# Score rows stored as single words, reciprocals on GpSimd, and 23 more products in three passes, in a four-layer graph network under a planned order

## The chip, the cores and the metric

The kernel runs on one core of one Trainium2 chip. Its time is the device time of one launch in microseconds. Before the change the median of three runs is 1486.99 us (1486.86 to 1487.59).

## What is computed

The input x has 32 graphs of 512 nodes with 128 features; one weighted adjacency matrix of 512 x 512 serves all graphs. Four layers follow each other, each of the form x = x + layer(relu(layernorm(x))). All of it is in fp32.

```python
# layer 0: graph convolution
A_norm = d[:, None] * (adj + I) * d[None, :];  out = (A_norm @ h) @ W.T + b
# layer 1: gated graph network, 5 steps; both of its matrices are adj
m_in = adj @ h;  av = concat([m_in, m_in]);  u3 = h @ u3_w.T + u3_b
z = sigmoid(av @ w3_w.T + w3_b + u3)
r = sigmoid(av @ w4_w.T + w4_b + u3)
hv = tanh(av @ w5_w.T + w5_b + (r * h) @ u5_w.T + u5_b)
h = (1 - z) * h + z * hv
# layers 2 and 3: graph attention
h = x @ W;  e = leaky_relu((h @ a_src)[:, None] + (h @ a_dst)[None, :])
alpha = softmax(where(adj > 0, e, -inf));  out = alpha @ h      # layer 2: elu(out)
```

## The kernel before

One graph's 512 x 128 tile is the unit: 128 partitions by four chunks of 128, 512 words in a partition, which is also one of the eight PSUM banks. Products come in two forms. A plain fp32 product (`weigh`, L829) is one call that the trace shows as two MATMUL records. A split product cuts both operands into an `upper` and a `lower` part and a scaled combination `across` of the two, held in the type float32r, and runs three single passes in place of one plain product (`one_pass`, L832; `in_three`, L713). The function `operands` (L683 to L692) makes the three parts of a tile: one ACT instruction for `upper` (L686), one DVE instruction for `lower` (L687) and one for `across` (L689). The parts have 5, 5 and 6 buffers. Between the first two passes and the third the partial sum in the bank is rescaled once by ACT (`rescale`, L695).

A step of layer 1 (`step`) starts a bank named `gate` with the state's product with the u3 weights and adds the message's product with the w4 weights. For the pairs (graph, step) that are in `STATE_GATES` (L31) the state's product too is run in three passes, with parts from `operands(hT, ...)`; for others it is one `weigh` from `hT`, issued with the third pass of the message. Steps 2 and 3 of the graphs 2 to 31 are in the set, and step 1 for graphs with b % 4 == 1: 67 products. The message's parts are made in every split step, so the rescaling of the bank is there in either case.

An attention layer of one graph (`gat`) normalises x, turns it through DRAM (`shuttle`), multiplies it by the weights with three score columns appended (L962), and takes the exponentials of the scores of two chunks at a time into the last three columns of `h_gat` (L978); ACT then scales the features by the first of them (L982). The column D + 2 of all 512 nodes is needed as a row in each partition. For graphs 0 to 27 DVE transposes the last 32 columns in 32 x 32 blocks into `four` (L998), one DMA issued by SP writes every 32nd partition of it to the DRAM tile `line` (L1000), and a second one reads `line` into all partitions of `row` (L1002). DVE multiplies and masks to the weights `e` (L1005, four instructions), and PE mixes the features with them (L1031), with the sum of the weights in the last column of each of two banks. DVE takes the reciprocals of two chunks' sums out of the bank (L1034) and ACT scales the bank by them into `v` (L1038); with that the bank is free. The last four graphs ("near") have their rows turned on PE and finish on DVE. A layer's result is added to x by an accumulating DMA that GpSimd issues (L658).

No loop sets the order. Every operation is first entered with `op(engine, cost, due, emit, r=, w=)`: an estimated cost, a due time, and what it reads and writes. `Plan.run` then simulates the engines as queues with these costs: a ready operation with the smallest due time starts when its engine is free and its buffers are there, and a buffer comes free with its last use. Ten rounds are made for each pair in the `ends` of the plan (L373), the best is kept, and `nudge` then moves due times by amounts that follow from the list `NUDGES`. The order in which operations started is the order in which each engine's instructions are emitted; on the chip each engine takes its instructions strictly in that order and waits by semaphores. SP (which issues nearly all DMAs) and GpSimd (POOL) are such queues too. So a changed cost, operation, end or nudge gives another order of the whole program.

Of the kernel before, what the change touches and what calls it, by code (L numbers as in the profile page):

```python
# [14 lines left out]
ALU = mybir.AluOpType  # L15

P = 128
# [3 lines left out]
W = 32  # L21
Q = P // W
# [5 lines left out]
RUN_UP = 8  # L28
LANES = 6
WHOLE_GATES = {(0, 0), (1, 0)}  # L30
STATE_GATES = {(b, s) for b in range(2, 32) for s in (1, 2, 3) if s > 1 or b % 4 == 1}  # L31

NUDGES = (
    53937, 420269, 836905, 654738, 2556, 688223, 875681, 275050, 155096, 344911, 330173, 435081, 694231, 213763,
    619624, 447574, 890946, 78316, 123147, 852796, 311235, 532539, 705019, 644762, 122001, 254734, 428857,
    882175, 724559, 991387, 688947, 809908, 194618, 494830, 529850, 799901, 343325, 398127, 50886, 241542,
    734658, 18633, 943566, 750849, 361157, 207391, 729651, 26139, 37696, 408480, 215591, 995383, 816582, 584268,
    494753, 34361, 342059, 302953, 168035, 239750, 279141, 68953, 280704, 389122, 194085, 766091, 380916,
    187191, 889942, 112078, 155070, 333073, 736484, 517839, 70535, 334845, 651590, 758394, 921455, 429200,
    648202, 752373, 775521, 430492, 606178, 231202, 882688, 679159, 354420, 928437, 520287, 661997, 81128,  # L40
    762603, 72380, 63081, 983120, 327354, 210125, 648122, 266391, 656086, 635831, 781379, 551997, 170768,
    229958, 7605, 122665, 19790, 73379, 142730, 998949, 708013, 923384, 153267, 690409, 481837, 535551, 726547,
    6387, 549650, 56134, 483951, 926497, 198992, 426418, 278155, 699450, 83978, 319322, 141756, 196198, 650583,
    862777, 201601, 166009, 204473, 988478, 570561, 164420, 526913, 618467, 275849, 776494, 261229, 110220,
    498182, 380461, 378001, 220860, 670765, 118796, 827070, 785629, 894747, 990151, 807156, 873672, 718913,
    239396, 50887, 63051, 862147, 532718, 800211, 505997, 9798, 801159, 13694, 618014, 193111, 44188, 893667,
    599496, 714567, 888600, 835938, 364887, 158288, 309678, 793120, 699620, 516755, 592013, 992036, 487540,
    190584, 971338, 58993, 486501, 268529, 250721, 557238, 569064, 166944, 933806, 390862, 463360, 136662,
    215430, 595978, 384591, 96926, 326923, 708222, 859934, 514585, 669817, 296375, 269747, 738262, 834297,
    459159, 608570, 133902, 490320, 941827, 144497, 573319, 819458, 309171, 845111, 880350, 927808, 432234,  # L50
    556385, 655493, 972795, 866892, 892882, 338341, 731096, 806800, 593721, 754374, 280850, 287395, 593450,
    812363, 340434, 322205, 340551, 845735, 66582, 645768, 736844, 878238, 109388, 497625, 999333, 437014,
    859840, 92294, 458622, 403652, 881921, 496809, 361450, 302403, 643048, 262383, 321316, 875159, 728173,
    763887, 249514, 200508, 52886, 149934, 537415, 299931, 655951, 358934, 513673, 678761, 726703, 828099,
    359414, 939210, 916234, 209320, 71814, 960653, 167324, 81204, 557783, 235008, 861486, 815903, 314980,
    593693, 811661, 356673, 912853, 833145, 889341, 728473, 302959, 14483, 119625, 907405, 192404, 98679, 42557,
    675297, 874633, 738462, 562610, 653446, 648327, 99334, 956314, 305909, 318958,
)


# [261 lines left out]
def gnn_stack(ctx: ExitStack, tc: tile.TileContext, a: dict, out: bass.AP):  # L322
    nc = tc.nc
    x, adj = a["x"], a["adj"]
    B, N, D = x.shape
    C = N // P
# [6 lines left out]
    def tiles(n, shape, name, pool=sb, dtype=F32):  # L333
        return [pool.tile(shape, dtype, name=f"{name}_{next(serial)}") for _ in range(n)]

    def flat(t):
# [19 lines left out]
        "hv": tiles(0, TOKENS, "hv"),  # L356
        "gT": tiles(0, [P, Q, W * C], "gT"),
        "h_gat": tiles(3, [P, C, D + 3], "h_gat"),
        "four": tiles(2, [P, Q, W], "four"),
        "row": tiles(2, [P, N], "row"),  # L360
        "line": tiles(4, [C, Q, W], "line", dram),
        "e": tiles(2, [P, C, N], "e"),
# [7 lines left out]
        "rstd": tiles(8, SMALL, "rstd"),  # L370
        "off": tiles(6, SMALL, "off"),
        "rden": tiles(3, SMALL, "rden"),
    }, [(167, 0.1), (181, 0.05)], 12,  # L373
        IDLE_FROM, lambda v: nc.tensor.transpose(v.t[:, 0, :], ident.t, ident.t))
    op = plan.op
    MM, MM1, TURN, MR = 0.858, 0.224, 0.111, 0.2325
# [44 lines left out]
    for c in range(C):  # L421
        e, q = (("ACT", nc.scalar), ("SP", nc.sync))[c % 2]
# [26 lines left out]
    for c in range(C):  # L449
        p = Val("bank")  # L450
# [90 lines left out]
    for i, l in enumerate((2, 3)):  # L541
        p = Val("bank")
# [398 lines left out]
    def gat(b, l, due):  # L941
# [45 lines left out]
        if near:  # L987
            pr = Val("bank")

            def spread():  # L990
                for k in range(Q):
                    nc.tensor.transpose(pr.t[:, k, :], h.t[:, k, D + 2:D + 3].to_broadcast([P, P]), ident.t)  # L992
            op("PE", C * TURN, due + 2, spread, r=[*exps, ident], w=[pr, e])
            row = pr
        else:

            four, line = Val("four"), Val("line")
            op("DVE", 0.2, due + 1.5, lambda: nc.vector.transpose(  # L998
                four.t, h.t[:, :, D + 3 - W:]), r=[h], w=[four])
            op("SP", 0.4, due + 1.5, lambda: nc.sync.dma_start(  # L1000
                line.t, four.t[W - 1::W]), r=[four], w=[line], delay=2.5)
            op("SP", 0.4, due + 1.5, lambda: nc.sync.dma_start(  # L1002
                row.t, line.t.rearrange("c q i -> (c q i)").unsqueeze(0).to_broadcast([P, N])), r=[line], w=[row, e], delay=7)
        for j in range(C):
# [4 lines left out]
        apart = near and l == 3 and b == B - 1  # L1009
        per = 1 if apart else 2  # L1010
        ps, rden, v, n = [Val("bank") for _ in range(C // per)], Val("rden", C), Val("y", 2), Val("r", 2)
        if near:

            def mix_from(js, cs):
                for j in js:
                    for c in cs:
                        nc.tensor.matmul(flat(ps[c // per].t).rearrange("p (c k) -> p c k", c=2)[:, c % per, :D + 1],  # L1017
                                         e.t[:, j, c * P:(c + 1) * P], h.t[:, j, :D + 1], start=j == 0 and c % per == 0,
                                         stop=j == C - 1, skip_group_check=True)
            for js, cs in [([j], range(C)) for j in range(2 if apart else C)] + [((2, 3), [c]) for c in range(C if apart else 0)]:  # L1020
                op("PE", len(js) * len(cs) * MM1, due + 4, lambda js=js, cs=cs: mix_from(js, cs),
                   r=[part for j in js for part in (e[j], h[j // 2], h[2 + j // 2])], w=[*ps] if len(js) == 1 else [ps[cs[0]]])
        for a, p in enumerate(ps):
            pt = lambda p=p: flat(p.t).rearrange("p (c k) -> p c k", c=2)
            chunks = range(per * a, per * a + per)
            some = slice(chunks[0], chunks[-1] + 1)
            for c in range(2 if not near else 0):
                def mix(a=a, c=c, pt=pt):
                    i = 2 * a + c
                    for j in range(C):  # L1030
                        nc.tensor.matmul(pt()[:, c, :D + 1], e.t[:, j, i * P:(i + 1) * P], h.t[:, j, :D + 1],  # L1031
                                         start=(j == 0), stop=(j == C - 1))
                op("PE", C * MM1, due + 4, mix, r=[e, h], w=[*ps] if a == c == 0 else [p])
            op("DVE", 0.08, due + 4, lambda some=some, pt=pt: nc.vector.reciprocal(rden.t[:, some], pt()[:, :per, D]), r=[p], w=[rden[c] for c in chunks])  # L1034
            if not near:
                def divide(chunks=chunks, pt=pt):
                    for c, i in enumerate(chunks):
                        nc.scalar.activation(v.t[:, i, :], pt()[:, c, :D], AF.Identity, bias=3.0 - l, scale=rden.t[:, i:i + 1])  # L1038
                op("ACT", 0.52, due + 4, divide, r=[p, *(rden[c] for c in chunks)], w=[v[a]])
            elif l == 2:  # L1040
                op("DVE", 0.335, due + 4, lambda some=some, pt=pt: nc.vector.tensor_mul(
                    v.t[:, some], pt()[:, :, :D], rden.t[:, some, None].to_broadcast([P, 2, D])), r=[p, rden[2 * a], rden[2 * a + 1]], w=[v[a]])
            else:
                def finish(chunks=chunks, pt=pt):
                    for c, i in enumerate(chunks):
                        nc.vector.scalar_tensor_tensor(xb.t[:, i, :], pt()[:, c, :D], rden.t[:, i:i + 1], xb.t[:, i, :],
                                                       op0=ALU.mult, op1=ALU.add)
                op("DVE", per * 0.26, due + 4, finish, r=[p, *(rden[c] for c in chunks)], w=[xb[c] for c in chunks])
# [77 lines left out]
```

## Time and profile before

| | |
|---|---|
| median of three runs | 1486.99 us |
| the profiled execution | 1487.39 us |
| its span, first to last instruction | 1485.6 us |
| granted TensorE clock | 1.000 |
| DMA packets on the hardware queue q1 | 276160, 41.6% of the 16 DMA engines' span |
| DMA packets on the software queue q0 | 30912, 16.3% |
| DMAs issued for `line`, each 2.0 KB | 56 |
| DMAs issued for `row`, each 256.0 KB | 56 |
| reciprocals out of two-chunk and one-chunk banks (L1034) | 130, 112 of them for graphs 0 to 27 |

The 1.8 us between the span and the time of the profiled execution lie outside the instructions. PE, DVE, ACT and POOL are the four computing engines; PEld is PE's weight load, which runs beside its matmuls. A MATMUL's duration in the records is not its cost, because matmuls are pipelined; the distance from one start to the next is.

### The profile page before, as it was taken

How to read it: one execution, taken by the hardware profiler on the slowest of the kernel's cores; microseconds unless marked ns; L12 is line 12 of the kernel's file. 1: busy time of each engine (PE TensorE's matmuls, PEld its weight loads, DVE VectorE, ACT ScalarE, POOL GpSimd, SP SyncE). 2: the span in 40 equal slices, each digit the busy share in tenths (PEclk: the TensorE clock that was granted, in tenths of full speed). 3: DMA queues.
4: the chain of work that ended last, by engine and by line, in shares of the span. 5: the costliest groups of instructions: out<-in, count | busy, mean ns of one | idle time of the engine just before them, and what ended most of it. 6: DMA issues, size and time to landing. Idle time of an engine off the chain costs nothing.

```text
span 1485.6 us, 25858 instructions
## 1 busy us (share of the span) xinstructions
PE 1478.1 (99%) x7481; PEld 1171.1 (79%) x7481; DVE 1406.2 (95%) x2951; ACT 1271.5 (86%) x2858; POOL 662.5 (45%) x1270
## 2 busy tenths in 40 slices
PE   9999999999999999999999999999999999999999
PEld 7777777787777788778778787877777877778888
DVE  8989999999998999899999999999999999999998
ACT  6978998888988888988889989799888889988874
POOL 5613641333755363655455553366536632414221
PEclk9999999999999999999999999999999999999999
DMA  3445555666766666666766557676576665553233
GB/s 107 65 104 144 108 127 117 139 142 159 154 136 134 156 156 138 139 142 138 178 138 145 134 128 153 143 173 139 127 162 154 148 158 122 136 135 74 70 79 79
DMA packets 307502, 196.12 MB, mean 132 GB/s; under 512 B 87872, under 2 KB 259232, under 8 KB 307360
## 3 DMA queue, kind: packets, MB, share of 16 engines
q1 hardware_dynamic: 276160, 157.24, 41.6%
q0 software_dynamic: 30912, 36.71, 16.3%
q8 instruction: 59, 0.97, 0.3%
q14 instruction: 83, 0.68, 0.2%
q10 hardware_dynamic: 288, 0.52, 0.1%
HBM read 87.30 MB, written 70.37 MB: 106 GB/s over the span
## 4 chain that ended last, share of the span: by engine, by line
PE 97%; DVE 1%; ACT 0%; DMA 0%; issue 0%; ACTq 0%; DVEq 0%
PE bank L713 35%; PE bank L832 26%; PE bank L829 15%; PE bank L1031 13%; PE bank L962 4%; PE bank L791 2%; PE bank L1017 2%; PE bank L736 1%; PE bank L653 0%; DVE e L1005 0%; DMA e<-in_adj_dram 0%; PE bank L507 0%; PE bank L992 0%; DVE st L630 0%; PE bank L455 0%
## 5 line engine op out<-in xcount | busy, mean ns | idle before, releaser
L695 ACT ACTIVATE bank<-bank 128x512 f32<-128x512 f32 x662 | 381.1, 598 | 92.4 <-PE bank L713 56.8
L689 DVE SCALAR_TENSOR_TENSOR across<-lower,upper 128x512 fp32r<-128x512 f32 x413 | 276.5, 678 | 2.2
L832 PE MATMUL bank<-upper,gates 128*128 128x512 f32 x541 | 257.2, 475 | 0.0
L1031 PEld LDWEIGHTS bank<-h_gat,e 128*128 128x128 f32 x1792 | 218.3, 191 | 17.6 <-issue 9.8
L1031 PE MATMUL bank<-h_gat,e 128*128 128x129 f32 x1792 | 220.5, 275 | 0.0
L832 PE MATMUL bank<-across,gates 128*128 128x512 f32 x541 | 218.3, 445 | 0.1
L832 PE MATMUL bank<-lower,gates 128*128 128x512 f32 x541 | 214.1, 396 | 0.0
L658 POOL DMA_DIRECT2D x<-y x80 | 72.1, 905 | 311.4 <-DVE y L1061 88.1
L713 PE MATMUL bank<-adj,upper 128*128 128x512 f32 x640 | 185.8, 412 | 0.0
L713 PE MATMUL bank<-adj,across 128*128 128x512 f32 x640 | 183.8, 411 | 0.0
L713 PE MATMUL bank<-adj,lower 128*128 128x512 f32 x640 | 172.7, 391 | 0.0
L829 PE MATMUL bank<-r,wT 128*128 128x512 f32 x320 | 163.3, 592 | 0.0
L1005 DVE SCALAR_TENSOR_TENSOR e<-row,h_gat,maskT 128x512 f32<-128x512 f32 x224 | 156.9, 741 | 0.0
L568 POOL TENSOR_TENSOR apart<-st 128x4 f32<-128x4 f32 x104 | 53.7, 517 | 218.1 <-DVE st L580 216.1
L713 PEld LDWEIGHTS bank<-adj,across 128*128 128x128 f32 x640 | 117.1, 188 | 36.6 <-issue 8.1
L713 PEld LDWEIGHTS bank<-adj,upper 128*128 128x128 f32 x640 | 117.8, 188 | 34.7 <-issue 10.3
L713 PEld LDWEIGHTS bank<-adj,lower 128*128 128x128 f32 x640 | 120.2, 188 | 26.6
L832 PEld LDWEIGHTS bank<-upper,gates 128*128 128x128 f32 x541 | 102.0, 188 | 42.5 <-issue 14.6
L832 PEld LDWEIGHTS bank<-across,gates 128*128 128x128 f32 x541 | 100.3, 188 | 41.1 <-issue 10.1
L874 ACT ACTIVATE r<-bank,gate_bw 128x512 f32<-128x512 f32 x160 | 111.4, 699 | 24.1 <-PE bank L829 21.4
L832 PEld LDWEIGHTS bank<-lower,gates 128*128 128x128 f32 x541 | 102.1, 189 | 37.8 <-issue 19.1
L568 POOL TENSOR_TENSOR rstd<-rstd,mhalf 128x4 f32<-128x4 f32 x104 | 128.1, 1232 | 5.1
(168 smaller groups left out, 3317.1 us busy)
## 6 DMA issues: line engine op xcount, KB each, us to landing
far<-sq SPq DMA_DIRECT2D x936, 64.0 KB
h<-far SPq DMA_DIRECT2D x148, 256.0 KB
x<-y POOLq DMA_DIRECT2D x80, 256.0 KB, 4.2
sq<-far SPq DMA_DIRECT2D x56, 256.0 KB
row<-line SPq DMA_DIRECT2D x56, 256.0 KB
adjT<-y POOLq DMA_DIRECT2D x32, 256.0 KB, 4.3
hT<-far SPq DMA_DIRECT2D x120, 64.0 KB
x<-in_x_dram SPq DMA_DIRECT2D x24, 256.0 KB
```

The source lines that it names most:

```text
L568: op("POOL", cost, due, lambda: nc.gpsimd.tensor_tensor(to(), one(), other(), how), r=r, w=w)
L658: op("POOL", 1.0, due, lambda: nc.gpsimd.dma_start(x.t, what(), accum_op=ALU.add), r=reads, w=[x], delay=7)
L689: op("DVE", V, due - 5, lambda: nc.vector.scalar_tensor_tensor(flat(across.t), flat(lower.t).bitcast(F32), -SPLIT, flat(upper.t).bitcast(F ...
L695: op("ACT", COPY, due, lambda: nc.scalar.mul(flat(p.t), flat(p.t), by), w=[p])
L713: nc.tensor.matmul(flat(p.t), left.t[:, c, :], right.t[:, c, :], start=first and c == 0, stop=c == C - 1, skip_group_check=True)
L791: nc.tensor.matmul(p.t[:, c, :], m.t[:, c, :], w0T.t[:, 0, :], start=True, stop=True)
L829: nc.tensor.matmul(flat(p.t), (of or gates).t[:, i, :], flat(moving.t), start=start, stop=True, skip_group_check=True)
L832: nc.tensor.matmul(flat(p.t), of.t[:, i, :], flat(moving.t), start=start, stop=True, skip_group_check=True)
L874: op("ACT", A, due - 5, lambda: nc.scalar.activation(flat(r.t), flat(gate.t), AF.Tanh, bias=gate_b["w4"].t, scale=0.5), r=[gate, gate_b["w ...
L962: nc.tensor.matmul(qt()[:, c, :D + 3], gT.t[:, 2 * a + c, :], w_aug[l].t, start=True, stop=True)
L1005: op("DVE", 0.661, due + 3, lambda j=j: nc.vector.scalar_tensor_tensor(e.t[:, j, :], matrix(row), h.t[:, j, D + 1:D + 2], mask.t[:, j, :], ...
L1031: nc.tensor.matmul(pt()[:, c, :D + 1], e.t[:, j, i * P:(i + 1) * P], h.t[:, j, :D + 1], start=(j == 0), stop=(j == C - 1))
```

## The change

Three things change, and the plan's ends and nudges with them.

1. `STATE_GATES` takes in step 1 for all graphs from 2 to 31: 90 products in place of 67. Each of the 23 new ones goes through `operands(hT, ...)` and three passes in place of one `weigh`.
2. The block transpose and `four` are gone. Four DMAs, one for each group of 32 partitions, take column D + 2 straight from `h_gat`, a word at a time (32 partitions by 4 words), into the four parts of `line`. They wait for the exponentials (`exps`) alone and not for the scaled features.
3. For graphs 0 to 27 ACT copies the two sums of a bank to an SBUF tile `den` (of the kind `ve`), GpSimd raises them to the power -1 into `rden`, and ACT's scaling waits for that. For the near graphs the DVE reciprocal stays.

```diff
-STATE_GATES = {(b, s) for b in range(2, 32) for s in (1, 2, 3) if s > 1 or b % 4 == 1}
+STATE_GATES = {(b, s) for b in range(2, 32) for s in (1, 2, 3)}
 NUDGES = (
-    53937, 420269, 836905, 654738, 2556, 688223, 875681, 275050, 155096, 344911, 330173, 435081, 694231, 213763,
...
+    527448, 875016, 948027, 354677, 457100, 447574, 546624, 346310, 530559, 796649, 845369, 700889, 705707,
...
-        "four": tiles(2, [P, Q, W], "four"),
...
-    }, [(167, 0.1), (181, 0.05)], 12,
+    }, [(156.9, 0.133)], 12,
...
-            four, line = Val("four"), Val("line")
-            op("DVE", 0.2, due + 1.5, lambda: nc.vector.transpose(
-                four.t, h.t[:, :, D + 3 - W:]), r=[h], w=[four])
-            op("SP", 0.4, due + 1.5, lambda: nc.sync.dma_start(
-                line.t, four.t[W - 1::W]), r=[four], w=[line], delay=2.5)
+            line = Val("line", C)
+            for c in range(C):
+                op("SP", 0.44, due + 1.5, lambda c=c: nc.sync.dma_start(
+                    line.t[c].rearrange("q i -> i q"), h.t[c * W:(c + 1) * W, :, D + 2]), r=exps, w=[line[c]], delay=3)
...
+        if not near:
+            den = Val("ve", 2)
...
-            op("DVE", 0.08, due + 4, lambda some=some, pt=pt: nc.vector.reciprocal(rden.t[:, some], pt()[:, :per, D]), r=[p], w=[rden[c] for c in chunks])
+            if not near:
+                op("ACT", 0.1, due + 4, lambda some=some, pt=pt: nc.scalar.copy(den.t[:, some], pt()[:, :per, D]), r=[p], w=[den[a]])
+                op("POOL", 1.15, due + 4, lambda some=some: nc.gpsimd.tensor_tensor(
+                    rden.t[:, some], den.t[:, some], minus1.t[:, some], ALU.pow), r=[den[a], minus1], w=[rden[c] for c in chunks], delay=1)
+            else:
+                op("DVE", 0.08, due + 4, lambda some=some, pt=pt: nc.vector.reciprocal(rden.t[:, some], pt()[:, :per, D]), r=[p], w=[rden[c] for c in chunks])
```

`NUDGES` is replaced as a whole by another list (315 numbers before, 186 after).

## The prediction

> **What bounds the kernel now.** I read the page's shares first, then the waits of PE, then the chain of waits, then the groups by shape, then the timeline where a duration was not a cost.
>
> ```profile
> PE 1478.1 (99%) x7481; PEld 1171.1 (79%) x7481; DVE 1406.2 (95%) x2951; ACT 1271.5 (86%) x2858; POOL 662.5 (45%) x1270
> PE 97%; DVE 1%; ACT 0%; DMA 0%; issue 0%; ACTq 0%; DVEq 0%
> ```
>
> PE is busy for all but 7.5 us and makes 97% of the chain that ended last; DVE is close behind with 95%. The waits of PE by itself begin like this, and its six rows sum to 4.0 us, most of it at the start:
>
> ```profile
> PE bank L411 <- DVE r L404: 1.1, 1, 1.1
> PE bank L1017 <- DVE e L1005: 0.9, 2, 0.6
> ```
>
> So the end moves with the sum of PE's passes and with nothing else, as long as PE stays fed. At most about 4 us can be won by a better order alone, and all of 4.0 plus any new wait can be lost. The chain of waits in a stretch of the middle gives the cost of each product:
>
> ```profile
> 603.66 0.86 PE bank L829 x2
> 604.52 0.48 PE bank L832 x2
> 605.86 1.86 PE bank L832 x8
> 608.66 1.87 PE bank L832 x8
> ```
>
> A plain product (two records) takes 0.86 us, a single pass 0.233. The groups by shape give the pieces that the change touches:
>
> ```profile
> L1034 DVE RECIPROCAL rden<-bank 128x2 f32<-128x2 f32 x126 | 18.0, 156 | 1.0 <-PE bank L1031 0.8
> L998 DVE STREAM_TRANSPOSE four<-h_gat 128x128 f32<-128x128 f32 x56 | 16.7, 298 | 2.9 <-ACT h_gat L982 2.9
> L978 ACT ACTIVATE h_gat<-bank 128x6 f32<-128x6 f32 x112 | 19.6, 190 | 4.9 <-PE bank L962 4.7
> L611 POOL TENSOR_TENSOR rstd<-rstd,mhalf 128x3 f32<-128x3 f32 x1 | 0.9, 866 | 5.8 <-DVE rstd L609 5.8
> L611 POOL TENSOR_TENSOR rstd<-rstd,mhalf 128x1 f32<-128x1 f32 x1 | 0.7, 682 | 0.0
> ```
>
> These means overlap from one instruction to the next. What an engine really gives to each is the distance of starts in the timeline of DVE:
>
> ```profile
> 310.16 0.30 DVE L998 STREAM_TRANSPOSE four<-h_gat 128x128 f32<-128x128 f32 x1
> 310.39 0.65 DVE L890 SCALAR_TENSOR_TENSOR hT<-r,r 128x512 f32<-128x512 f32 x1
> ...
> 312.75 0.68 DVE L687 TENSOR_TENSOR lower<-hT,upper 128x512 fp32r<-128x512 f32 x1
> 313.35 0.68 DVE L687 TENSOR_TENSOR lower<-h,upper 128x512 fp32r<-128x512 f32 x1
> 313.95 0.68 DVE L890 SCALAR_TENSOR_TENSOR hT<-r,r 128x512 f32<-128x512 f32 x1
> ```
>
> A block transpose costs 0.23 us, a 512-wide instruction 0.60. A reciprocal at 1468.95 is followed by the next start at 1469.03: 0.08. DVE's margin by stage:
>
> ```profile
> 600.00:800.00 200.00, 200.00 (x986) 157.57 (x986) 190.50 (x375) 178.18 (x399) 104.69 (x197) 1.00 0.65 146
> 1200.00:1400.00 200.00, 200.00 (x978) 156.40 (x977) 193.02 (x372) 175.11 (x388) 59.70 (x116) 1.00 0.49 119
> ```
>
> The fourth figure is DVE: 7 to 10 us free in 200, ACT (the fifth) 22 to 25, POOL about half.
>
> **What the Trainium skill says.** "FP8 and Floating Point Precision", TensorE Precision Notes, has a true fp32 product as four passes; the trace agrees (0.86 is 3.7 passes of 0.233). "PSUM — Partial Sum Buffer", The four PSUM rules, says that GpSimd cannot touch PSUM; so the sums must first be copied by ACT, and no row of this trace has a POOL instruction on a bank. "DMA: Bandwidth & Descriptors", Rules for kernel authors, says that a strided last dimension becomes one descriptor per element; the word columns will then be 512 packets for a row, which no run here shows yet. "Perfetto Trace Analysis", GPSIMD Engine Instruction, calls POOL's spans unreliable and the spacing of starts better; the trace agrees (spans on POOL overlap at 608.15 to 610.82).
>
> **Part 1, 23 products in three passes.** On PE each removes 0.86 and adds 3 x 0.233 = 0.70: 0.16 saved, 3.7 us in all. Taken over the whole span, L832 has 26% of 1485.6 us for 3 x 541 passes, 0.238 each, which includes small gaps: 0.146 saved, 3.4 us. I take 0.152: **3.5 us off PE's sum**, and since PE is the chain, off the end. The price is 23 more instructions on ACT (0.51 each by starts at 619.84 and 620.35: 11.7 us) and 46 on DVE (0.60 each: 27.6 us). The rescaling of the bank is there already. The parts need one more set of upper, lower and across buffers per product: 436 sets in place of 413 (DVE's L689 has x413), 6% more turnover.
>
> **Part 2, words in place of the transpose.** DVE loses 56 x 0.23 = 12.9 us. SP has 224 issues where it had 56, 168 more at 0.43 (128 words a piece at 8.5 to 14 us) to 0.50 (L1000): 72 to 84 us. It issues some 1,440 DMAs now, at about 0.46 some 660 us, so it goes from 45 to 50% of the span. Behind the four issues on SP stand the writes and reads of the shuttles, each 1.5 us later than it could be at most, 56 times. The wait moves from DVE's transpose (SP stands 81.3 us for it in 22 waits) to the exponentials, which ACT ends a scaling earlier, so SP is held less. The packets are 56 x 512 = 28,672 more. The queue's mean packet costs 41.6% x 16 x 1485.6 / 276160 = 0.036 us of one DMA engine; at that price they add 64 us to the 16 engines' mean, 4% of the span; at the least almost nothing. I take 2%. The row arrives within about a microsecond of when it did: three more issues (1.4 us) against the transpose, its wait and the scaling saved. DVE never stood idle ahead of L1005, so I cost the row at nothing; the six interleaved graphs of work hide it. If that cover were gone, 56 x 1 us would be the scale.
>
> **Part 3, reciprocals by GpSimd.** DVE loses 112 x 0.08 = 9.0 us. DVE in sum: 27.6 - 12.9 - 9.0 = +5.7 us of 79 free: it gets no closer to being the bound (95.0%). ACT gets 112 copies of 128 x 2 out of a bank, like L978: between 0.05 (starts 620.35, 620.40) and 0.19 each, 6 to 21 us; with part 1 it goes from 1271 to about 1296, 87%. POOL gets 112 powers of two columns; L611 with one and three columns brackets them at 0.68 and 0.87, I take 0.78: 87 us, 45 to 51%. The bank waits for copy, power and scaling in place of reciprocal and scaling: at least 1 us longer. At 621.66 the reciprocal is done and the scaling starts at 623.39, since ACT has other work queued, so 1 us fits into waits that are there now. New waits: POOL's power stands for ACT's copy, and behind it norms and accumulating DMAs; ACT's scaling stands for POOL, and behind it ACT's rescalings (L695), for which PE waits.
>
> **The new order.** Other ends and nudges reshuffle everything. Below: it could win up to 3 us of the 4.0 that PE waits, not the start. Above: no reason excludes a loss. I take nothing, because the plan's costs matched the chip well enough in the kernel before to leave PE hardly a wait between 50 and 1400 us, and the same costs stand in the new plan.
>
> **The sum.** 1487.39 (profiled) - 3.5 = 1483.9; the profiled execution lies 0.4 above the median, so the forecast for the median is **1483.5**, 0.24% less. About 0.2%, 3.0 us, is what a measurement of this kernel tells from no change; the line is at 1484.0, close to my forecast.
>
> **Rivals.**
> 1. PE loses part of the gain to small waits. For: DVE and ACT both get fuller, with 23 more sets of parts in unchanged buffers. Against: there is no such wait now. With 0.5 to 6.5 us of waits, 1484.0 to 1490.0; at 2.5, 1486.0.
> 2. ACT is held at its scaling by GpSimd. POOL's norm runs as a string of ten instructions, from 624.65 to 631.45 in the timeline, and POOL stands up to 34 us for the data of an accumulating DMA (L658). A power queued behind either comes late, ACT stands, the rescalings behind it come late, and PE stands for the third pass. For: ACT already waits 14.2 us for the reciprocals of DVE. Against: POOL is half idle and the order is made with its queue in it. If one scaling in ten (11 of 112) costs PE 1 us, 1483.5 + 11 = 1494.5. It decides for slower from 6.5 us of PE waits on, 58 ns for each reciprocal.
> 3. The order gets tighter as well: 3.5 + 2.5 less, 1481.0. For: DVE is rid of 168 instructions that broke its rows. Against: PE has no wait left to give in the middle.
> 4. The change doesn't do what it says because plain products stay in the trace: then 1487.0. The diff leaves no room for it.
>
> **How the numbers follow.** The forecast with PE as full as now 0.46, rival 1 0.28, rival 2 0.22, rival 3 0.04, rival 4 nothing. Faster is forecast and rival 3, 0.50; within 0.2% is rival 1, 0.28; slower is rival 2, 0.22. The forecast's own range is 1482.5 to 1484.0 (the bounds of 0.146 and 0.16 per product and a spread of 0.5). The range to hold 8 in 10 goes from 1480.5, below rival 3, over all of rival 1 to 1491.5, into the mild third of rival 2; some 0.15 is left out above.
>
> **What would show it.** L829 from hT falls from x186 by 46 records to x140, and L832 rises from x541 to x564 for each part. PE's busy time falls by 3 to 4 us and its share stays at 99%. DVE stays at 95%; POOL goes to about 51%. ACT's waits for `rden` on POOL stay below some 30 us in all; if they are above 60 us and PE's waits grow, rival 2 is right. Waits of PE on parts (L686 to L689) or on `e` speak for rival 1. Packets of 4 bytes on q1 rise by 28,672 with less than 5% more share. I am wrong if PE's waits exceed 8 us, or if its passes take another time than 0.86 and 0.233.

## The result, and the profile after

The changed kernel takes 1627.8 us, median of four runs (1621.63 to 1633.24), beside 1487.2 us (1486.86 to 1487.59) for the kernel before: a ratio of 1.0945, 95% interval 1.0918 to 1.0971. It is 140.6 us slower, where 3.5 us less had been forecast. The profiled execution has 1626.86 us and a span of 1625.0. Line numbers in the changed code are about ten less than before (the third pass L832 is now L822, the plain product L829 is L819, the DMA that reads the row L1002 is L991).

These are the shares, the main DMA queue and the chain's shares, from the page of the changed kernel:

```profile
PE 1523.2 (94%) x7502; PEld 1197.1 (74%) x7502; DVE 1416.1 (87%) x2829; ACT 1293.4 (80%) x2993; POOL 751.9 (46%) x1382
...
q1 hardware_dynamic: 307968, 157.25, 41.5%
...
PE 19%; DMA 17%; ACT 7%; DVE 7%; SPq 5%; issue 2%; DVEq 0%; ACTq 0%
```

PE made 97% of the chain. Now the chain can be followed back only to 697.85 us, so its shares sum to 57% of the span; PE makes 19 of these and DMA 17. No engine has become the bound: all four have a smaller share than PE had, DVE and ACT smaller ones than their own before. The share that might have warned, that of the DMA engines, is where it was (41.6%). But it is a share of a longer span: as busy time, 41.6% of 1485.6 us are 618 us and 41.5% of 1625.0 are 674. PE's busy time grew by 45 us, although the new products should have made it 3.5 us less. The clock, which was granted at 0.98 over the span and at 1.000 before, may have a part in that: two per cent of 1625 us, 32 us, is an upper estimate.

In the two stretches by stage that the prediction used (us, then PE, PEld, DVE, ACT, POOL, the clock, the DMA share, GB/s) PE, DVE and ACT are emptier, POOL is fuller, in one stretch the clock falls to 0.95, and less is moved in a microsecond than before (129 and 117 GB/s for 146 and 119):

```profile
600.00:800.00 200.00, 188.10 (x915) 147.03 (x914) 175.17 (x328) 164.34 (x380) 116.23 (x196) 0.98 0.65 129
1200.00:1400.00 200.00, 177.87 (x807) 136.52 (x806) 165.94 (x307) 149.82 (x338) 80.16 (x166) 0.95 0.54 117
```

The waits of PE (us in total, times, longest) were six rows with 4.0 us in all. Now 22 rows make about 98 us, and they begin like this:

```profile
PE bank L952 <- DMA sq<-far: 19.4, 10, 5.3
PE bank L819 <- DMA hT<-far: 14.7, 3, 7.0
PE bank L822 <- ACT bank L685: 13.5, 8, 4.1
```

PE waits for data from the shuttles through DRAM, which the change did not touch, and for ACT, which waits for such data in its turn. So look at the queue that issues all these transfers. The waits of SP in the changed kernel:

```profile
SPq L991 <- DMA line<-h_gat: 169.3, 63, 6.7
...
SPq L989 <- ACT h_gat L968: 55.7, 21, 11.3
```

SP stands 169.3 us ahead of the row's DMA (L991) until the words have landed in `line`. In the kernel before the same wait, for a block in place of words, was 22.4 us in 18 waits:

```profile
SPq L1002 <- DMA line<-four: 22.4, 18, 2.6
```

The timeline of SP in the changed kernel shows one such row:

```profile
452.49 1.64 SPq L989 DMA_DIRECT2D line<-h_gat  x3
454.18 0.43 SPq L657 DMA_DIRECT2D far<-sq  x1
454.66 0.85 SPq L989 DMA_DIRECT2D line<-h_gat  x1
455.55 0.47 SPq L408 DMA_DIRECT2D x<-in_x_dram  x1
462.85 0.34 SPq L991 DMA_DIRECT2D row<-line  x1
```

The last of the four word DMAs is issued by 455.51, and the read of the row only at 462.85. In between SP issues nothing for 6.8 us. In the kernel before, the read of a row came 2.80 us after the block's DMA, with four other issues between:

```profile
216.00 0.62 SPq L1000 DMA_DIRECT2D line<-four  x1
...
218.80 0.40 SPq L1002 DMA_DIRECT2D row<-line  x1
```

But SP's standing is not all. The chain that ended last (start, us, what) holds transfers of other tiles as long as that:

```profile
768.91 7.67 DMA h<-far
...
798.21 7.20 DMA line<-h_gat
826.71 7.34 DMA line<-h_gat
...
871.21 7.44 DMA hT<-far
```

`h<-far` and `hT<-far` are plain shuttle reads. Either the words slow down whatever is under way with them, or these reads were merely issued into a crowd. That became the question for the experiments, beside the two others that the prediction left: GpSimd's reciprocals and the order.

### The profile page after: what moved, and what is told of

Same layout as the page of the kernel before. It is cut to its first block, busy times and chain, and to the rows that moved or that the text cites. A ratio compares the mean times of both kernels' runs of the same rounds, so it can differ in the third digit from the quotient of the medians.

```text
span 1625.0 us, 26265 instructions
## 1 busy us (share of the span) xinstructions
PE 1523.2 (94%) x7502; PEld 1197.1 (74%) x7502; DVE 1416.1 (87%) x2829; ACT 1293.4 (80%) x2993; POOL 751.9 (46%) x1382
## 3 DMA queue, kind: packets, MB, share of 16 engines
q1 hardware_dynamic: 307968, 157.25, 41.5%
## 4 chain that ended last, share of the span: by engine, by line
PE 19%; DMA 17%; ACT 7%; DVE 7%; SPq 5%; issue 2%; DVEq 0%; ACTq 0%
DMA line<-h_gat 7%; PE bank L703 5%; PE bank L822 5%; PE bank L1022 3%; DMA h<-far 3%; PE bank L819 3%; DMA far<-sq 2%; PE bank L1008 2%; ACT bank L685 2%; DMA hT<-far 1%; SPq L657 1%; DMA row<-line 1%; DVE lower L677 1%; SPq L989 1%; PE bank L952 1%
## 5 line engine op out<-in xcount | busy, mean ns | idle before, releaser
L679 DVE SCALAR_TENSOR_TENSOR across<-lower,upper 128x512 fp32r<-128x512 f32 x436 | 290.7, 678 | 4.0 <-PE bank L822 1.4
L822 PE MATMUL bank<-upper,gates 128*128 128x512 f32 x564 | 264.9, 470 | 6.6 <-ACT bank L685 2.8
L822 PE MATMUL bank<-across,gates 128*128 128x512 f32 x564 | 225.2, 446 | 19.4 <-ACT bank L685 10.7
L1022 PEld LDWEIGHTS bank<-h_gat,e 128*128 128x128 f32 x1792 | 226.6, 195 | 19.3 <-issue 5.5
L822 PE MATMUL bank<-lower,gates 128*128 128x512 f32 x564 | 227.1, 403 | 9.6 <-DVE lower L677 9.6
L1022 PE MATMUL bank<-h_gat,e 128*128 128x129 f32 x1792 | 230.6, 279 | 1.9 <-DVE e L994 1.9
L703 PE MATMUL bank<-adj,across 128*128 128x512 f32 x640 | 191.5, 425 | 10.8 <-ACT bank L685 10.5
L1027 POOL TENSOR_TENSOR rden<-ve,minus 128x2 f32<-128x2 f32 x112 | 106.2, 977 | 179.4 <-ACT ve L1026 176.2
L819 PE MATMUL bank<-r,wT 128*128 128x512 f32 x320 | 164.2, 595 | 2.4 <-DVE r L866 2.4
L676 ACT ACTIVATE upper<-h 128x512 fp32r<-128x512 f32 x158 | 100.6, 638 | 69.0 <-DMA h<-far 63.2
L558 POOL TENSOR_TENSOR apart<-st 128x4 f32<-128x4 f32 x104 | 70.3, 677 | 179.8 <-DVE st L570 179.1
L822 PEld LDWEIGHTS bank<-across,gates 128*128 128x128 f32 x564 | 105.1, 192 | 60.2 <-ACT bank L685 20.0
L677 DVE TENSOR_TENSOR lower<-h,upper 128x512 fp32r<-128x512 f32 x158 | 107.2, 680 | 45.7 <-ACT upper L676 43.4
L822 PEld LDWEIGHTS bank<-upper,gates 128*128 128x128 f32 x564 | 108.2, 192 | 52.3 <-ACT bank L685 14.6
L822 PEld LDWEIGHTS bank<-lower,gates 128*128 128x128 f32 x564 | 108.3, 192 | 50.1 <-issue 16.5
```

Of the source, the lines that this page charges most:

```text
L558: op("POOL", cost, due, lambda: nc.gpsimd.tensor_tensor(to(), one(), other(), how), r=r, w=w)
L676: op("ACT", COPY, due - 5, lambda: nc.scalar.mul(made(upper.t), given(src.t), BELOW), r=[src], w=[upper])
L677: op("DVE", V, due - 5, lambda: nc.vector.tensor_sub(made(lower.t), given(src.t), made(upper.t).bitcast(F32)), r=[src, upper], w=[lower])
L679: op("DVE", V, due - 5, lambda: nc.vector.scalar_tensor_tensor(flat(across.t), flat(lower.t).bitcast(F32), -SPLIT, flat(upper.t).bitcast(F ...
L703: nc.tensor.matmul(flat(p.t), left.t[:, c, :], right.t[:, c, :], start=first and c == 0, stop=c == C - 1, skip_group_check=True)
L819: nc.tensor.matmul(flat(p.t), (of or gates).t[:, i, :], flat(moving.t), start=start, stop=True, skip_group_check=True)
```

## The experiments

**Theories.** A: a DMA of single words takes long to land, and that alone (times 56, through SP and through what waits) makes the loss. B: GpSimd holds ACT at its scaling (the prediction's second rival). C: the planned order no longer fits, since it was made with a landing of 3 us for the words. Within A: is it the number of words, of DMAs, or the place they are written to; and is it SP's wait or the transfers themselves?

**Landing alone.** A kernel of its own that computes no layer; it stores a row in several ways on SP's queue and reads it back with a DMA that must wait for the store, once with idle DMA engines and once behind eight 64 KB stores of ACT's queue. A DMA has landed when its semaphore says that all of it has arrived; SP issues the read only then, so the time from issue to issue measures the landing.

```python
sync.dma_start(line["block"], four[W - 1::W])                                       # L55, 4 runs of 512 B
sync.dma_start(line["one"][0].rearrange("q i -> i q"), S[:W, :, D + 2])              # L60, 128 words
sync.dma_start(line["few"][0, :, :4].rearrange("q i -> i q"), S[:4, :, D + 2])       # L76, 16 words
```

> No layer is computed; the output is the input. The kernel only stores scores to DRAM in several forms, each followed by a read of what was stored, which SP can issue only when the store has landed; eight times each, first with nothing else under way, then behind eight 64 KB DMAs of another queue. Words theory: the block form (4 runs of 512 B) lands in about 2 us as before, one DMA of 128 single words in clearly more, four of them in 6 to 7 us or more, and 16 words are as fast as the block; then the number of single words is the cost. Rival, the number of DMAs: one DMA of 128 words lands like the block, and four only 1.5 us later (three more issues). Rival, GpSimd: all forms land in about 2 us and the 6 us seen in the changed kernel come from queueing behind other DMAs, so they show only in the loaded half.

The timeline of SP in this kernel, each store with the read after it:

```profile
31.06 0.50 SPq L55 DMA_DIRECT2D lineblock<-four  x1
32.64 0.32 SPq L56 DMA_DIRECT2D R<-lineblock  x1
...
57.71 0.32 SPq L60 DMA_DIRECT2D lineone<-S  x1
64.79 0.32 SPq L61 DMA_DIRECT2D R<-lineone  x1
```

From issue to issue the block takes 1.66 us (median), one DMA of 128 words 6.4 (5.5 to 8.0), the four of a row 7.9 from the first and 6.6 from the last, 16 words 1.2, and 32 runs of 16 bytes 1.66. The eight big stores beside them change no median by more than 0.53 us. So the landing of words takes 4.7 us longer than a block's by itself, without contention (4.2 beside the stores), and it doesn't add up over four DMAs: they land together.

**The changed kernel with fewer words.** Its order, queues and number of DMAs are kept; each word DMA moves 16 words in place of 128, and the rest of the row holds leftovers (GpSimd writes them once at the start, here and in the later runs with leftovers).

```diff
-  line.t[c].rearrange("q i -> i q"), h.t[c * W:(c + 1) * W, :, D + 2])
+  line.t[c][:, :4].rearrange("q i -> i q"), h.t[c * W:c * W + 4, :, D + 2])
```

> The changed kernel with its order kept to the instruction, and each of the four score DMAs moving 16 words in place of 128; the other words of the row are leftovers, so the weights are computed from other numbers. SP's queue, its waits on the exponentials and the number of DMAs stay. Words theory: SP stands some 10 us for line in place of 169 us, and the time falls to 1484 to 1500 us. Rival, the four DMAs themselves and the ring of DMA semaphores: 1580 to 1630 us. Rival, GpSimd's reciprocals hold ACT: 1600 to 1630 us with ACT's and POOL's waits as they are.

It takes 1488.76 us in one run, with 1487.78 for the kernel before beside it. Its page, and SP's wait ahead of the row:

```profile
PE 1476.7 (99%) x7502; PEld 1176.0 (79%) x7502; DVE 1410.0 (95%) x2829; ACT 1290.5 (87%) x2993; POOL 777.0 (52%) x1386
...
SPq L992 <- DMA line<-h_gat: 11.0, 22, 1.4
```

With the same 224 DMAs, the same GpSimd reciprocals, the same 90 products and the same nudged order, the whole loss but about a microsecond is gone. That leaves little to B, and to C only what the order can't stand once words land late.

**Each part alone, both in an order without nudges.** The kernel before with `NUDGES = ()` is their base; one adds the words, the other the reciprocals by copy and GpSimd, and both keep the 67 products.

> The kernel before with an empty list of nudges: what an order costs that has not been nudged, as the base for the parts that are run alone without nudges. All theories: 1495 to 1515 us.

> The kernel before, without nudges, with the score row as single words alone (reciprocals on DVE, 67 products in three passes). Words theory: 100 to 150 us more than the kernel before without nudges, 1600 to 1660 us, with SP standing over 120 us for line. Rival, GpSimd's reciprocals: within 15 us of the kernel before without nudges.

> The kernel before, without nudges, with the reciprocals of graphs 0 to 27 by copy on ACT and power on GpSimd alone (row through the block transpose, 67 products). Words theory: within 10 us of the kernel before without nudges, 1494 to 1514 us, ACT standing less than 30 us for the reciprocals. Rival, GpSimd's queue holds ACT's scalings and with them PE: 10 us and more above it, over 1514 us.

One run each: the base 1504.3 us, with words 1635.0 (+130.7), with GpSimd's reciprocals 1507.05 (+2.75, but taken on another chip than the base). With the words SP's wait ahead of the row is large again, if a little under the 120 us expected:

```profile
SPq L975 <- DMA line<-h_gat: 111.4, 38, 6.5
```

Dropping the nudges alone costs 16.5 us, so the order is worth something, but an order without nudges loses about as much to the words as the nudged one. In the kernel with GpSimd's reciprocals, the waits around the tile `rden`, and ACT's among those who waited for it:

```profile
  POOL rden L1013: 0.2, 1
```

ACT stood 0.2 us in all for GpSimd's power. B falls as the cause of 140 us; that the reciprocals cost a microsecond or two is not excluded.

**What makes words slow: the place.** Again a kernel without layers: one DMA of words, then the read that must wait for it, by number and by distance in DRAM.

```python
sync.dma_start(tight[0, :, :8].rearrange("q i -> i q"), S[:8, :, D + 2])         # L53, 32 words, also 2, 16 and all 32 partitions
sync.dma_start(by64[:, :, 0].rearrange("q i -> i q"), S[:W, :, D + 2])           # L69, 128 words 64 B apart
```

> No layer is computed; the output is the input. One DMA of single words from SBUF to DRAM and a read of the place behind it, which SP issues when the words have landed, eight times for each form, with nothing else under way. First 8, 32, 64 and 128 words in one block of 512 B (columns of four rows), then 128 words with the four of a partition next to each other, then 128 words 64 B apart, then 128 words 512 B apart, last 128 words the other way, from DRAM to SBUF. Theory that the words wait for each other in one place in DRAM: the time to land grows with the count, by some 0.04 us a word (8 words 1.2 us, 32 some 2.2, 64 some 3.7, 128 some 6.3), and 128 words 512 B apart land in 2 us or less. Rival, that a word costs by itself wherever it goes: 6 to 7 us at 64 B and 512 B apart too. From DRAM to SBUF 128 words take about 2 us by the first theory, 6 by the second.

Medians from issue to the read's issue: 8 words 1.08 us, 32 words 1.18, 64 words 2.77, 128 words in one block of 512 bytes 6.26 (5.85 to 6.64), 128 words with four of a partition adjacent 6.93. But 128 words 64 bytes apart 1.39, 512 bytes apart 1.38, and 128 words read from DRAM into SBUF 1.99. The timeline of SP, for 32 words, 128 words, and 128 words 64 bytes apart:

```profile
44.97 0.27 SPq L53 DMA_DIRECT2D tight<-S  x1
46.14 0.34 SPq L54 DMA_DIRECT2D R<-tight  x1
...
158.66 0.30 SPq L61 DMA_DIRECT2D tight<-S  x1
164.76 0.34 SPq L62 DMA_DIRECT2D R<-tight  x1
...
320.57 0.32 SPq L69 DMA_DIRECT2D by<-S  x1
321.97 0.26 SPq L70 DMA_DIRECT2D R<-by  x1
```

The same 128 packets of 4 bytes land in 1.4 or in 6.3 us, by nothing but how close together they are written. But closeness alone is not slow either: 32 words, and the 32 runs of 16 bytes that filled the same 512 bytes, took 1.18 and 1.66. It takes many packets in one place. A growth in proportion to the words was expected and is not there: up to 32 there is hardly any, and from 64 to 128 it more than doubles.

**The place alone, in the changed kernel.** All 512 words in the same four DMAs and the same order; in DRAM each word gets 64 bytes of its own, and the words of one DMA are 256 bytes apart. The row's DMA reads the first 2 KB, which are then mostly leftovers, so that it costs what it did.

```diff
+    lines = tiles(4, [Q, W, C, 16], "line", dram)
-  line.t[c].rearrange("q i -> i q"), h.t[c * W:(c + 1) * W, :, D + 2])
+  line.t[:, :, c, 0].rearrange("q i -> i q"), h.t[c * W:(c + 1) * W, :, D + 2])
...
-  row.t, line.t.rearrange("c q i -> (c q i)")...
+  row.t, line.t.rearrange("q i c k -> (q i c k)")[:N]...
```

> The changed kernel with its order kept to the instruction and all 512 words of a row moved by the same four DMAs, but into a DRAM tile in which each word has 64 B of its own; the row is read from the first 2 KB of that tile, so most of what the weights are computed from is leftovers. Same packets, same issues, same waits. Theory of words that wait for each other in one place: 1484 to 1490 us, SP standing under 30 us for line. Rival, that single words cost by their number: 1600 to 1630 us. Rival, queues and DMA semaphores: 1580 to 1630 us.

1492.0 us (1490.66 to 1493.33, seven runs) against 1487.86; ratio 1.0026, interval 1.0016 to 1.0037, a little above the 1484 to 1490 us expected. So 135.8 of the 140.6 us (1627.8 less 1492.0) come with the place where the words land. A kernel that reads all 512 words back from so wide a tile was not run. SP's waits and its timeline at one row:

```profile
SPq L992 <- DMA line<-h_gat: 16.6, 19, 3.0
```

```profile
603.48 1.88 SPq L990 DMA_DIRECT2D line<-h_gat  x4
...
608.04 0.63 SPq L992 DMA_DIRECT2D row<-line  x1
```

The wait that was 169.3 us is 16.6. And on the page of this kernel the last figure of a line, the median time from issue to landing, is short again:

```profile
h<-far SPq DMA_DIRECT2D x148, 256.0 KB, 3.0
...
hT<-far SPq DMA_DIRECT2D x120, 64.0 KB, 2.6
```

Such reads took 7.67 and 7.44 us where the chain of the changed kernel met them; the chain meets the slow ones, and a median of that kernel is not on its page. The busy time of q1 is 630 us here (42.3% of 1489.4), 44 us less than with the same packets written tightly.

**Is it SP's wait?** The row's DMA reads a spare tile that no word is written to. SP then need not wait for words ahead of the row; everything else stays, the words too.

```diff
-  row.t, line.t.rearrange("c q i -> (c q i)")...
+  row.t, spare.rearrange("c q i -> (c q i)")...
```

> The changed kernel with its order kept to the instruction and all word DMAs as they are, but the row is read from a DRAM tile that no word is written to, so SP does not wait for the words ahead of a row; the weights are computed from leftovers. Theory that SP standing ahead of the row is the harm: 1484 to 1500 us. Rival, that the words also stop what is queued behind them, in the engines or by the semaphores: still over 1540 us, with the 169 us of waits ahead of the row gone and other waits for line larger.

1665.24 us in one run, slower still (before beside it 1488.65). Its waits of SP:

```profile
SPq L660 <- DMA far<-sq: 121.2, 114, 7.2
...
SPq L658 <- DMA line<-h_gat: 55.6, 30, 5.5
```

SP is spared most of the row's wait (20.5 us are left) and stands at the shuttles instead: for `far<-sq`, up to 7.2 us at a time (79.7 us and at most 4.0 before the edit). SP's wait ahead of the row is where the loss showed, and not what made it.

**What the words do to others.** A kernel without layers: a 64 KB store in 32 runs of 2 KB (the expectation says 512 bytes; the packets have 2 KB), to a tile of its own in DRAM, and the read that waits for it; alone, behind four tight word DMAs, behind four whose words are 64 bytes apart, and on ACT's queue beside SP's words.

```python
words(tight)                          # L42, on SP's queue
other.dma_start(far[:W], load[:W])    # L68, on ACT's queue
other.dma_start(R[:W, :], far[:W])    # L69
```

> No layer is computed; the output is the input. A 64 KB store to DRAM in runs of 512 B and a read of it that is issued when it has landed: alone on SP's queue; behind four tight word DMAs (those of the change) on SP's queue; behind four word DMAs with 64 B for each word; alone on ACT's queue; on ACT's queue behind four tight word DMAs of SP's; then a read inside SBUF alone and behind the words; last eight 32 KB stores behind the words on SP's queue. Theory that slow words stop the DMA engines for what is queued behind them: alone some 2 us from issue to landing, behind tight words on the same queue 5 us or more, behind words apart 2 us; on the other queue as slow if the engines themselves stand, as fast as alone if only the queue does. Rival, that words harm only who waits for them and SP's ring of semaphores: 2 to 2.5 us behind the words too, and only the last form is slow, because SP cannot issue its fifth store and later until the words have landed.

Medians from the store's issue to the read's: alone 1.60 us on SP's queue and 1.64 on ACT's; behind tight words on the same queue 7.59 (7.22 to 7.91); behind words set apart 1.67; on ACT's queue, with the tight words on SP's, 7.48 (7.32 to 8.60). The timeline of SP, alone and behind tight words, and then that of ACT's queue beside words, with two stretches of it (the last two figures are the DMA engines' share and GB/s):

```profile
11.38 0.30 SPq L49 DMA_DIRECT2D far<-load  x1
12.98 0.30 SPq L50 DMA_DIRECT2D R<-far  x1
...
48.08 0.37 SPq L54 DMA_DIRECT2D far<-load  x1
55.65 0.31 SPq L55 DMA_DIRECT2D R<-far  x1
```

```profile
217.31 0.32 ACTq L68 DMA_DIRECT2D far<-load  x1
224.85 0.31 ACTq L69 DMA_DIRECT2D R<-far  x1
...
217.30:219.90 2.60, 0.00 (x0) 0.00 (x0) 1.00 0.22 26
219.90:224.85 4.95, 0.00 (x0) 0.00 (x0) 1.00 0.00 0
```

While tight words land, a store from another queue to another place lands late too. What is late in the record is the landing and not the moving: 26 GB/s in the first stretch are the 64 KB of the store and the words, and in the 4.95 us that follow no packet of anything moves, until the store counts as landed and its read is issued. Nor does it take a target in DRAM. A 256 KB copy inside SBUF on SP's queue, alone and behind tight words, has these times from issue to landing:

```profile
DMA to landing us min/median/max: 2.2/2.3/2.6
...
DMA to landing us min/median/max: 5.9/6.3/7.3
```

In the changed kernel, where more is under way, single packets are held too: by the trace's packet records the longest of 2 KB took 5.63 us there, 1.20 in the kernel before and 1.69 with the words set apart. What holds packets and landings back, in the engines or in the memory behind them, is not shown.

Eight stores of 32 KB behind the words show a second way in which words harm. The read after them is issued 7.74 us after the first store, so the 6 us are lost once and not eight times; but SP needs 7.0 us to issue the eight, because it stands for the words at the later ones (32.9 us in 16 waits over the eight repetitions). These stores take nothing from the words' tile. The trace shows why SP waits all the same: its DMAs use eight semaphores in turn, and one may have to wait until the eighth before it has landed. This was the rival's mechanism, and it is real, also in the changed kernel, where SP stands 32.3 us for `line` ahead of the shuttles' writes (L657). It is not the whole: the store on ACT's queue waits for no such turn and is late. How the 135.8 us divide between late landings and SP's turns is not separated.

**Would an order that knows help?** The changed kernel planned with the words' landing at 7 us (`delay=7` in place of 3), with an end and nudges of its own.

> The changed kernel with the plan told that a word DMA takes 7 us to land in place of 3; words, reciprocals and 90 products as in the change; ends (149.1, 0.113) and nudges found for it. Theory that the harm is a landing which the order did not know of, since SP takes its queue strictly in order: 1486 to 1500 us although every word still takes 6 to 7 us to land, and SP standing under 40 us for line. Rival, that slow words harm however they are ordered (more DMAs in flight, semaphores held for longer): over 1530 us.

1658.22 us (1653.93 to 1662.31, four runs), ratio 1.1145, interval 1.1124 to 1.1167: the expectation fell. Its waits of SP:

```profile
SPq L643 <- DMA line<-h_gat: 59.5, 33, 4.0
```

Of SP's waits for `line`, that at the row is down to 58.0 us, and the one at the shuttles' writes (L643) is as large. A plan that puts other transfers between the words and their row puts them where nothing lands. This fits the run with the spare tile, and C falls in the form in which it was put. The plan's model has a delay for the words, but no way to say that others land late; an order that knows that was not tried.

**The two other parts without the words.** The changed kernel with 90 products and GpSimd's reciprocals, the row through block transpose and `four` as before, with an end and nudges of its own.

```diff
-            line = Val("line", C)
-            for c in range(C):
-                op("SP", 0.44, due + 1.5, ...
...
+            four, line = Val("four"), Val("line")
+            op("DVE", 0.2, due + 1.5, lambda: nc.vector.transpose(four.t, h.t[:, :, D + 3 - W:]), r=[h], w=[four])
+            op("SP", 0.4, due + 1.5, lambda: nc.sync.dma_start(line.t, four.t[W - 1::W]), r=[four], w=[line], delay=2.5)
```

> The changed kernel with the row through the block transpose and one DMA, as before the change; the 90 products and the reciprocals by copy and GpSimd stay; ends (157.6, 0.191) and nudges found for this list of operations. Words theory with my working for the other two parts: 3.5 us less than the kernel before, 1482 to 1486 us; DVE then has 18.6 us more than before and the order need not be as tight, so up to 1489 us. Rival, GpSimd's reciprocals or the fuller DVE cost PE waits: 1490 us or more.

1489.63 us (1487.13 to 1493.15, 15 runs); ratio 1.0012, interval 1.0004 to 1.0019. Its page:

```profile
PE 1476.7 (99%) x7502; PEld 1176.0 (79%) x7502; DVE 1420.8 (95%) x2885; ACT 1292.2 (87%) x2993; POOL 785.7 (53%) x1382
```

That is just above the 1489 us that the theory allowed and just below the 1490 of its rival. PE's busy time is 1.4 us less than before the change, and the time is 1.8 us more (against 1487.86): the passes saved are lost again between them. Its list of nudges has 41 numbers, that of the kernel before 315, and dropping all of these cost 16.5 us; so a longer search for its order may be worth the difference, which was not tried. No version tried beats the kernel before.

## Why the prediction was wrong, point by point

The step that failed is the one in part 2: "The row arrives within about a microsecond of when it did ... so I cost the row at nothing". The row comes some 5 us later than that (7.9 us from the first of four word DMAs to the row's read, 1.66 for a block), and the size of this term is not the worst of it: while the words land, other transfers land late as well. "If that cover were gone, 56 x 1 us would be the scale" missed both. As an estimate, 56 rows by about 6 us (7.59 less 1.60) are 336 us of late landings; 135.8 us, 2.4 us for a row, came through. That the six interleaved graphs hid the rest is argued and not shown. The price was taken from the queue's mean packet, as busy time of the DMA engines: 64 us at most. That busy time did grow, by 56 us, but that is luck: 44 of them are gone when the same packets are written apart, so they are not what the words' own packets cost. The Trainium skill's "DMA: Bandwidth & Descriptors", Rules for kernel authors, was read rightly for the count (one packet for each word), and the same page's Specifications say that a transfer under 512 bytes is written by read-modify-write. Here 128 words of 4 bytes need 1.39 us or 6.26 by their place, so the size alone prices nothing; that many such writes to one small place go one after the other would fit, but no run shows that mechanism.

The other steps:

- **Part 1.** The counts came as stated, 140 records from `hT` and 564 of each third of the split product. No run had this part alone. The prices held: in the run with few words the chain again has 0.86 us for a plain product (1011.16) and 1.40 for six passes (1001.48). But PE's busy time fell by 1.4 us there and not by 3 to 4, and nothing of the gain reaches the end.
- **DVE and ACT.** DVE was forecast 5.7 us fuller and stays at 95% where the words don't disturb (1410.0 us with few words, 3.8 more). ACT was forecast at 1296 us and has 1293.4.
- **SP.** 224 issues with a median of 0.43 us less 56 of 0.50 make 69 us, near the 72 to 84. Its largest wait ahead of the words fell from 81.3 to 55.7 us, as argued.
- **Part 3.** GpSimd was forecast 87 us fuller and is 89.4; that is luck, since it is 114.5 fuller with few words, where nothing is disturbed. A power has 977 ns and not 780, but spans on POOL overlap. The groups by shape of the changed kernel show it, with ACT's scaling and its copy:

```profile
L1027 POOL TENSOR_TENSOR rden<-ve,minus 128x2 f32<-128x2 f32 x112 | 106.2, 977 | 179.4 <-ACT ve L1026 176.2 <-ACT bank L685 2.1 <-ACT h_gat L968 0.7
L1034 ACT ACTIVATE y<-bank,rden 128x128 f32<-128x128 f32 x224 | 70.2, 384 | 4.8 <-POOL rden L1027 4.6
L1026 ACT COPY ve<-bank 128x2 f32<-128x2 f32 x112 | 17.9, 172 | 15.6 <-PE bank L1022 15.2
```

  The scaling stood 4.6 us for GpSimd, in 224 instructions, against the bound of 30. The second rival is refuted as the cause, here and in the run with GpSimd's reciprocals alone. It had the right sign and nothing else.
- **The new order.** "I take nothing" was off by some 5 us. With few words the kernel should have been at 1487.78 - 3.5 = 1484.3 and has 1488.76; with the row as before it should have been at 1484.4 and has 1489.63. This is the first rival, at the upper end of its 0.5 to 6.5 us: small waits of PE, on ACT and on shuttles, no group of them over 2.3 us in all, and a PE whose busy time falls by less than its passes. With ACT at 87% in place of 86%, with 23 more sets of parts, and in an order with fewer nudges, which of the three makes them was not separated.

Two of the prediction's own signs did their work: PE's waits above 8 us, and its share below 99%. The sign that it set for the words (packets up by 28,672, share up by less than 5%) would have passed the kernel as sound: the packets are up by 31,808, of which the words are 28,672, and the share is not up at all.

The clock fell to 0.967 to 0.98 in each kernel whose words land tightly and stood at 0.998 or above in every other kernel with the layers. It goes with a PE that keeps standing and starting (98 us of waits in place of 4.0). Whether it adds to the loss, within the 32 us at most, is not shown.

## What to carry to other kernels

A DMA costs its issue, its packets' time on the engines, and its landing; a changed shape or place of the written bytes can change the last alone, four- to fivefold (1.39 to 6.26 us here), with the first two as they were, so before a row of small writes goes into a kernel, measure from its issue to the issue of a read that depends on it. Ask too what stands behind it in all queues, since no share of busy time showed here that transfers landed late. When a loss shows as one engine's wait, take the wait away and see whether the time comes back: here it moved to the next transfer.

## What was not expected of the hardware

- 128 words of 4 bytes that one DMA writes into one block of 512 bytes of DRAM land in 6.26 us, 64 of them in 2.77, 32 in 1.18; 128 words that are 64 or 512 bytes apart land in 1.4, and one block of 4 runs of 512 bytes in 1.66. The Trainium skill's "Perfetto Trace Analysis", DMA Instruction — HWDGE (DVE, Sync), says of the confirmation of a write that it "can cause a surprisingly long delay especially when the write target is HBM"; the trace agrees (128 words from DRAM to SBUF took 1.99), but shows that for words it hangs on their place and number.
- While four such DMAs land, a 64 KB store from another queue to another place needs 7.48 us in place of 1.64, though all its packets have moved some 5 us before; a copy inside SBUF on the same queue needs 6.3 in place of 2.3.
- Four such DMAs in a row land together, 7.9 us after the first, and the DMA engines' busy share of the span shows none of it: 41.6% before, 41.5% after, with 31,808 packets more.
